# A perceiver block in one program: the folded queries on halves of the array's rows, the value products alternating between halves of its columns

## The chip, the cores and the metric

The kernel runs on one core of one Trainium2 chip. The metric is the device time of one execution in microseconds (us), taken over several executions; beside it stands one execution recorded by the hardware profiler. All data are fp32.

## What is computed

The reference is a two-layer perceiver on a latent `x` of 16 x 64 x 256 with a context of 16 x 1601 x 256: a cross attention that gathers samples, a self attention, a mixture of 8 experts, then a second cross attention, a state-space scan and a mixture of 32 experts. The change lies in the second cross attention alone:

```
def _L1_xattn_ref(x, context, Wq, Wk, Wv, Wk_ip, Wv_ip, Wo, bo):
    HEADS, DIM_HEAD, TEXT_LEN, SCALE = 16, 64, 77, 64 ** (-0.5)
    ctx_txt = context[:, :TEXT_LEN, :]
    ctx_img = context[:, TEXT_LEN:, :]                       # 1524 rows
    q = (x @ Wq).reshape(B, N, HEADS, DIM_HEAD)              # N = 64
    k = (ctx_txt @ Wk).reshape(B, TEXT_LEN, HEADS, DIM_HEAD)
    v = (ctx_txt @ Wv).reshape(B, TEXT_LEN, HEADS, DIM_HEAD)
    out = _attend(q, k, v)
    k_ip = (ctx_img @ Wk_ip).reshape(B, Li, HEADS, DIM_HEAD)
    v_ip = (ctx_img @ Wv_ip).reshape(B, Li, HEADS, DIM_HEAD)
    out_ip = _attend(q, k_ip, v_ip)
    out = out + out_ip
    return out @ Wo + bo
...
x = x + _L1_xattn_ref(_layernorm(x, axis=-1), ctx_1024, ...)
```

`_attend` is a softmax of `q k^T * SCALE` over the context rows, times `v`.

## The kernel before

**No keys and no values of the image rows are formed.** For a head, `q k^T = q Wk_ip^T ctx^T`, so the kernel first multiplies the 64 queries of the head with the head's 64 rows of `Wk_ip` and gets a folded query with 256 features ("fold"). The scores are then products of the raw context with the folded query. In the same way the probabilities are first multiplied with the raw context, which gives 256 features per query, and only then with the head's 64 columns of `Wv_ip` ("out").

**Tiling.** There are 16 batches and 16 heads. Two heads are taken together as a pair `hp`, with their 2 x 64 queries side by side as 128 columns. So there are 128 steps `n` (16 batches x 8 pairs). A step has 12 chunks of 128 context rows (the last has 116).

**One step (`Cross.step`, L1051), in the order in which TensorE (PE) gets it.** PE, VectorE (DVE) and ScalarE (ACT) work strictly in the order in which the Python code emits the work; nothing reorders it.

1. Three times, a PSUM bank `st` is filled with the scores of four chunks (L1068): 8 matmuls each, with the turned context `cT` as the stationary operand and the folded query `qf` as the moving one. DVE takes the maximum over the chunks (L1071, L1073). Between the second and the third bank, the normalised result of step n-2 is transposed (`turn_out`, L1042).
2. `out(n - 2)` (L1079): six matmuls into one bank `py`. Each head has a text product (77 rows of `vt` against `ptt`) and two image products (`wvi` against `ot`, one for each half of the 256 features). A head's `lhsT` has 64 columns, so head 0 uses the left half of the array's columns and writes partitions 0 to 63 of the bank, and head 1 the right half and partitions 64 to 127. All three products of head 0 are emitted, then all three of head 1.
3. The products of step n-1's probabilities with the context, in three parts of four chunks each (`product`, L1034). Between parts 0 and 1 stands the transpose of the maxima (L1088), between parts 1 and 2 the transpose that spreads them over all partitions (L1098) and, straight after it, `fold(n + 1)` (L1102).
4. ACT copies the spread maxima to `mc` (L1100) and the folded query to `qf` (L999); DVE subtracts `mc` from the three `st` banks (L1109, L1112) and ACT takes the exponentials (L1110, L1113). `qf` is needed by the first score matmul of step n+1.

**The fold.** `qbd` holds the scaled queries as a block diagonal: partitions 0 to 63 are the features of head 0 and are nonzero only in the columns of head 0's queries; partitions 64 to 127 and head 1 likewise. The other two blocks were set to zero once. A fold is therefore two full matmuls (128 rows, 128 columns, 128 moving columns), one for each half of the 256 features, into one bank, and one ACT copy of 256 columns.

**PSUM.** There are eight banks in two rings of four. `bank()` hands out the ring that nearly everything uses. `big()` hands out the ring of the score banks (L144); in this stage only L1065 takes from it, three a step. A bank that is handed out again must first have been read by all its readers; for a score bank the last of them is the subtraction on DVE (L1109, and for the third bank L1112).

**Around it.** Other work is woven into the steps by generators that are advanced at fixed places (`tick`, `mid`, `side`): the last gathers of the first cross attention, the self attention, the experts of the first layer, the state-space scan and the routing of the second layer.

An fp32 matmul shows in the trace as two passes, each with its own weight load. Where a row counts "x12" for `out`, these are the two passes of six matmuls; a fold is four passes.

Of the kernel before, what the change touches and what calls it, by code (L numbers as in the profile page):

```python
# [17 lines left out]
P = 128  # L18
B, S, D = 16, 64, 256
M = 1601  # L20
KC = D // P
# [13 lines left out]
H1, HD1, INNER, TEXT = 16, 64, 1024, 77  # L35
# [29 lines left out]
def perceiver_kernel(ctx: ExitStack, tc: tile.TileContext, a: dict, out: bass.AP):  # L65
    nc = tc.nc

    def mk(pool, shape, tag, dtype=F32, bufs=None):
        return pool.tile(list(shape), dtype, tag=tag, name=tag, bufs=bufs)
# [15 lines left out]
    def mm(o, pairs):  # L85
        for i, (l, r) in enumerate(pairs):
            nc.tensor.matmul(o, lhsT=l, rhs=r, start=i == 0, stop=i == len(pairs) - 1)  # L87
# [53 lines left out]
    def bank():  # L141
        return mk(pmm, [P, 512], "mm")

    def big():  # L144
        return mk(psc, [P, 512], "st")
# [9 lines left out]
    def load(pool, tag, src, shape, bufs=None):  # L155
        t = mk(pool, shape, tag, bufs=bufs)
        nc.sync.dma_start(out=t, in_=src)
        return t
# [46 lines left out]
    for t in range(TG):  # L205
        z = mk(const, [P, P], f"att{t}")
# [9 lines left out]
    qbds = [mk(xw, [P, NHP, 2, 2, S], f"qbd{i}") for i in range(2)]  # L216
# [50 lines left out]
    for j in range(2):  # L267
        r = slice(j * S, (j + 1) * S)
# [619 lines left out]
    class Cross:  # L888
# [98 lines left out]
        def fold(self, n):  # L987

            if n >= B * NHP:
                return  # L990
            b, hp = divmod(n, NHP)
            w = self.w[b, hp // 4]
            rhs = qbds[b // 2 % 2][:, hp, b % 2].rearrange("p h q -> p (h q)")
            pf = bank()
            for k in range(KC):
                nc.tensor.matmul(pf[:, k * P : (k + 1) * P], lhsT=w[:, hp % 4, k * P : (k + 1) * P], rhs=rhs,  # L996
                                 start=True, stop=True)
            qf = self.qf[n] = mk(self.xp, [P, KC, P], "qf", bufs=2)
            nc.scalar.copy(qf.rearrange("p c n -> p (c n)"), pf[:, : KC * P])  # L999

        def out(self, n):

            if n < 0:
                return
            b, hp = divmod(n, NHP)
            t, bb = divmod(b, 2)
            if t not in self.yt:
                self.yt[t] = mk(self.xp, [P, NHP, 2, S], "yt", bufs=2)
            ot = self.ot.pop(n)
            py = bank()  # L1010
            for h in range(2):
                r = slice(h * HD1, (h + 1) * HD1)
                cols = slice(hp * P + h * HD1, hp * P + (h + 1) * HD1)
                mm(py[r, :S], [(self.vt[b][:TEXT, cols], self.ptt[b][:TEXT, hp, r])]
                   + [(wvi[:, k, cols], ot[:, k, r]) for k in range(KC)])
            nc.scalar.copy(self.yt[t][:, hp, bb, :], py[:, :S])  # L1016

        def project(self, t):
# [484 lines left out]
    with tc.manual_schedule(engines={ET.PE, ET.DVE, ET.Activation}):  # L1503
# [43 lines left out]
        wvi = load(xw, "wvi", a["xwvi"].rearrange(kp, p=P), [P, KC, INNER])  # L1547
# [51 lines left out]
        i = 0  # L1599
# [104 lines left out]
```

## Time and profile before

| What | us |
|---|---|
| median of 10 executions | 3090.1 |
| lowest and highest of them | 3081.74 and 3097.48 |
| the profiled execution, its own time | 3084.45 |
| its span in the trace | 3082.6 |
| PE busy in the span | 2866.4 (93%) |
| stretch in which the 128 steps of the cross attention lie | about 850 to 2790 |

In rows of instructions, a form such as `128*64 128x64` stands for a matmul whose stationary operand covers 128 rows and 64 columns of the array and whose moving operand has 128 partitions and 64 columns. PEld is the loading of stationary operands, which has its own row and overlaps the matmuls. "Chain" rows give the start of a piece in us, its length, and what it was. The mean granted TensorE clock of the execution was 0.974 of full speed.

### The profile page before, as it was taken

The page shows a single profiled execution, that of the slowest core. Times are in us where ns is not written, and L with a number is a line of the kernel's source. Part 1 is how long each engine was busy: PE and PEld are TensorE (multiplying, and loading weights), DVE is VectorE, ACT ScalarE, POOL GpSimd, SP SyncE. Part 2 cuts the span into 40 slices and gives each one's busy share as a digit, 9 for nine tenths or more (in the row PEclk, how much of TensorE's full clock was granted, in tenths as well). Part 3 has the DMA queues.
Part 4 walks back from the last instruction along what each step waited for, and adds up shares of the span by engine and source line. Part 5 has one row for each costly group of instructions (what it writes and reads, how often), then busy time and mean ns, then how long its engine had stood idle before and what let it go on. Part 6 is the DMA issues. An engine that isn't in the chain of part 4 may idle for free.

```text
span 3082.6 us, 46371 instructions
## 1 busy us (share of the span) xinstructions
PE 2866.4 (93%) x17710; PEld 2367.0 (77%) x17710; DVE 1620.4 (53%) x4126; ACT 1017.3 (33%) x2353; POOL 809.3 (26%) x919
## 2 busy tenths in 40 slices
PE   7799999968799999988899999999999999998879
PEld 4454445646688898867799999999899999996666
DVE  3421223234365666655533457765686587656756
ACT  2343444312223223234233343333342433223421
POOL 0275446555345555200000000100020011002621
PEclk9899999988899999999999999999999999999999
DMA  6499876653312122120155221111121122004983
GB/s 210 116 191 197 241 210 192 182 145 109 111 28 71 30 68 70 47 70 31 61 164 189 66 73 50 60 53 53 35 84 56 38 68 69 8 1 153 287 234 114
DMA packets 338710, 326.19 MB, mean 106 GB/s; under 512 B 59301, under 2 KB 289097, under 8 KB 337977
## 3 DMA queue, kind: packets, MB, share of 16 engines
q1 hardware_dynamic: 186473, 226.04, 24.0%
q10 hardware_dynamic: 126640, 62.79, 7.7%
q0 software_dynamic: 25376, 34.39, 5.3%
q8 instruction: 141, 2.31, 0.3%
q14 instruction: 80, 0.66, 0.1%
HBM read 248.90 MB, written 74.22 MB: 105 GB/s over the span
## 4 chain that ended last, share of the span: by engine, by line
PE 77%; DVE 12%; DMA 5%; ACT 2%; issue 2%; POOL 1%; SPq 0%; ACTq 0%; DVEq 0%; POOLq 0%
PE st L87 32%; PE mm L1040 20%; PE mm L87 16%; PE mm L152 5%; DMA wg<-in_guT 2%; PE mm L996 2%; DMA tab<-kv 1%; PE mm L1026 1%; DVE mp L1071 1%; PE mm L965 1%; DMA cx<-in_ctx 1%; DVE pt L1109 1%; DVE hs L1275 1%; DMA g<-tab,ig 1%; PE mm L1088 1%
## 5 line engine op out<-in xcount | busy, mean ns | idle before, releaser
L427 POOL DMA_INDIRECT g<-tab,ig x640 | 610.9, 955 | 638.2 <-DVE ig L425 442.8
L1040 PE MATMUL mm<-cn,pt 128*128 128x257 f32 (+1 forms) x3072 | 740.5, 384 | 0.0
L87 PE MATMUL st<-qf,cT 128*128 128x128 f32 x6144 | 735.7, 277 | 0.9 <-ACT qf L999 0.9
L87 PEld LDWEIGHTS st<-qf,cT 128*128 128x128 f32 x6144 | 716.9, 193 | 5.9 <-ACT qf L999 2.4
L1040 PEld LDWEIGHTS mm<-cn,pt 128*128 128x128 f32 (+1 forms) x3072 | 554.0, 190 | 81.6 <-issue 0.8
L1071 DVE TENSOR_REDUCE mp<-st 128x128 f32<-128x512 f32 x384 | 260.7, 688 | 232.4 <-PE st L87 232.0
L87 PE MATMUL st<-wkv,cxt 128*128 128x512 f32 (+1 forms) x832 | 380.5, 602 | 0.6 <-ACT cxt L396 0.6
L1109 DVE TENSOR_TENSOR pt<-st,mc 128x512 f32<-128x512 f32 (+1 forms) x384 | 224.2, 640 | 133.4 <-ACT mc L1100 133.4
L87 PEld LDWEIGHTS st<-wkv,cxt 128*128 128x128 f32 (+1 forms) x832 | 151.0, 190 | 160.0 <-issue 158.1
L1110 ACT ACTIVATE pt<-pt 128x512 f32<-128x512 f32 (+1 forms) x384 | 208.1, 588 | 61.2 <-DVE pt L1109 60.9
L380 ACT COPY kv<-st 128x512 f32<-128x512 f32 (+1 forms) x208 | 120.9, 587 | 217.1 <-PE st L87 195.8
L1100 ACT COPY mc<-mm 128x128 f32<-128x128 f32 x128 | 34.1, 266 | 352.4 <-PE mm L1098 351.9
L1049 ACT COPY ot<-mm 128x256 f32<-128x256 f32 x128 | 47.5, 371 | 310.2 <-PE mm L152 309.7
L1090 DVE TENSOR_REDUCE xmx<-mm 128x1 f32<-128x128 f32 x128 | 37.4, 292 | 191.9 <-PE mm L1088 191.9
L87 PE MATMUL mm<-xt,w 128*128 128x256 f32 x512 | 122.8, 394 | 3.9 <-DVE act L815 3.8
L1281 POOL TENSOR_TENSOR ys<-ys,hc 128x512 f32<-128x512 f32 x64 | 81.5, 1274 | 161.1 <-DVE hc L1280 161.0
L87 PEld LDWEIGHTS mm<-xt,w 128*128 128x128 f32 x512 | 101.0, 199 | 28.8 <-issue 9.3
L1365 POOL DMA_INDIRECT xb<-xnd,row x55 | 55.2, 1004 | 241.6 <-PE mm L1026 199.8
L1016 ACT COPY yt<-mm 128x64 f32<-128x64 f32 x128 | 27.2, 213 | 253.5 <-PE mm L87 253.5
L459 DVE TENSOR_REDUCE smx<-sc 128x4 f32<-128x20 f32 x32 | 5.4, 168 | 167.4 <-ACT sc L457 167.4
L901 POOL MEMSET cn<- 128x12 f32 x16 | 1.8, 120 | 338.0 <-PE mm L1040 295.8
L815 DVE TENSOR_TENSOR act<-gl,mm 128x256 f32<-128x256 f32 x64 | 26.4, 418 | 107.6 <-ACT gl L814 107.5
(441 smaller groups left out, 3978.1 us busy)
## 6 DMA issues: line engine op xcount, KB each, us to landing
tab<-kv ACTq DMA_DIRECT2D x48, 1024.0 KB
w<-in_gate SPq DMA_DIRECT2D x62, 512.0 KB
cx<-in_ctx SPq DMA_DIRECT2D x48, 512.0 KB
cn<-in_ctx SPq DMA_DIRECT2D x16, 1408.0 KB
wg<-in_guT SPq DMA_DIRECT2D x87, 256.0 KB
wk<-in_xwkiT SPq DMA_DIRECT2D x32, 512.0 KB
w<-in_lin SPq DMA_DIRECT2D x31, 512.0 KB
wd<-in_down1T SPq DMA_DIRECT2D x87, 128.0 KB
```

Source lines behind the costliest of these rows:

```text
L87: nc.tensor.matmul(o, lhsT=l, rhs=r, start=i == 0, stop=i == len(pairs) - 1)
L152: nc.tensor.transpose(t[:ncol, i, :rows], b, ident[:rows, :rows])
L380: nc.scalar.copy(kv[:w, :, c, :], pk[:w].rearrange("p (h e) -> p h e", h=H0))
L427: nc.gpsimd.indirect_dma_start(out=gf[:, (half * n + s) * 4 * HD0 : (half * n + s + 1) * 4 * HD0], out_offset=None, in_=tables[j], in_offs ...
L996: nc.tensor.matmul(pf[:, k * P : (k + 1) * P], lhsT=w[:, hp % 4, k * P : (k + 1) * P], rhs=rhs, start=True, stop=True)
L1040: nc.tensor.matmul(po, lhsT=pt[:w, c, :], rhs=cn[:w, c, :], start=c == 0, stop=c == NCH - 1)
L1049: nc.scalar.copy(ot, tp[:, :KC, :])
L1071: nc.vector.tensor_reduce(mp_[:, i, :], s.rearrange("p c n -> p n c"), AX.X, ALU.max)
L1109: nc.vector.tensor_tensor(o, st[i][:, :m, :], mc.to_broadcast([P, m, P]), ALU.subtract)
L1110: nc.scalar.activation(o, o, AF.Exp)
L1281: nc.gpsimd.tensor_tensor(y, y, hc, ALU.add)
L1365: nc.gpsimd.indirect_dma_start(out=x, out_offset=None, in_=xnd, in_offset=bass.IndirectOffsetOnAxis(ap=tb.row[:, i : i + 1], axis=0))
```

## The change

`fold` and `out` are rewritten; nothing else differs.

```
         def fold(self, n):
...
-            rhs = qbds[b // 2 % 2][:, hp, b % 2].rearrange("p h q -> p (h q)")
-            pf = bank()
+
+            pf = [z[:, : KC * S].rearrange("p (k q) -> p k q", q=S) for z in (bank(), big())]
             for k in range(KC):
-                nc.tensor.matmul(pf[:, k * P : (k + 1) * P], lhsT=w[:, hp % 4, k * P : (k + 1) * P], rhs=rhs,
-                                 start=True, stop=True)
+                for h in range(2):
+                    r = slice(h * HD1, (h + 1) * HD1)
+                    nc.tensor.matmul(pf[h][:, k, :], lhsT=w[r, hp % 4, k * P : (k + 1) * P],
+                                     rhs=qbds[b // 2 % 2][r, hp, b % 2, h, :], start=True, stop=True)
             qf = self.qf[n] = mk(self.xp, [P, KC, P], "qf", bufs=2)
-            nc.scalar.copy(qf.rearrange("p c n -> p (c n)"), pf[:, : KC * P])
+            for h in range(2):
+                nc.scalar.copy(qf[:, :, h * S : (h + 1) * S], pf[h])
 
         def out(self, n):
...
             py = bank()
+            pairs = []
             for h in range(2):
                 r = slice(h * HD1, (h + 1) * HD1)
                 cols = slice(hp * P + h * HD1, hp * P + (h + 1) * HD1)
-                mm(py[r, :S], [(self.vt[b][:TEXT, cols], self.ptt[b][:TEXT, hp, r])]
-                   + [(wvi[:, k, cols], ot[:, k, r]) for k in range(KC)])
+                pairs.append([(self.vt[b][:TEXT, cols], self.ptt[b][:TEXT, hp, r])]
+                             + [(wvi[:, k, cols], ot[:, k, r]) for k in range(KC)])
+
+            for i in range(KC + 1):
+                for h in range(2):
+                    l, m = pairs[h][i]
+                    nc.tensor.matmul(py[h * HD1 : (h + 1) * HD1, :S], lhsT=l, rhs=m, start=i == 0, stop=i == KC)
             nc.scalar.copy(self.yt[t][:, hp, bb, :], py[:, :S])
```

In `fold`, the two full matmuls become four: for each half of the features one for each head, with that head's 64 rows of the array, all 128 columns and 64 moving columns. The zero blocks of `qbd` are no longer read here (the text scores still read them). The two heads write two banks, one from each ring, so the ring of the score banks now hands out four banks a step. The one ACT copy of 256 columns becomes two of 2 x 64 columns, one for each bank.

In `out`, the same six matmuls are emitted in another order: text product of head 0, text product of head 1, then the two image products in the same alternation.

## The prediction

> **What bounds the kernel now.** I read the page's busy shares first, then the busy time by stretches, then the chain of waits inside one step, and last the order of time around the two places that change.
>
> ```profile
> PE 2866.4 (93%) x17710; PEld 2367.0 (77%) x17710; DVE 1620.4 (53%) x4126; ACT 1017.3 (33%) x2353; POOL 809.3 (26%) x919
> ```
>
> ```profile
> 1180.00:1500.00 320.00, 288.99 (x2019) 258.32 (x2018) 187.59 (x539) 103.23 (x247) 51.93 (x62) 0.96 0.18 55
> ...
> 1840.00:2300.00 460.00, 457.42 (x3426) 420.77 (x3425) 312.34 (x663) 167.22 (x410) 39.04 (x62) 1.00 0.19 58
> 2300.00:2790.00 490.00, 484.81 (x3578) 443.14 (x3577) 317.02 (x746) 161.67 (x398) 29.38 (x45) 1.00 0.12 38
> ```
>
> Columns: stretch, its length, busy us of PE, PEld, DVE, ACT, POOL, then the granted clock. In the second half of the cross attention PE is busy for 457.4 of 460.0 and 484.8 of 490.0 us at full clock. The loosest stretch (1180 to 1500) still has 289 of 320. So what the change adds to PE's own time in a step, or takes from it, reaches the end nearly whole, 128 times. In the chain of one step (start, length, what):
>
> ```profile
> 1508.75 1.79 PE st L87 x16
> 1510.54 0.66 PE mm L87 x12
> 1511.20 1.94 PE mm L1040 x8
> ...
> 1515.43 0.11 PE mm L1098
> 1515.54 0.45 PE mm L996 x4
> 1515.99 1.74 PE mm L1040 x8
> ```
>
> Everything here is PE. Sixteen full passes take 1.79, that is 0.112 each. The fold (L996) is four such passes, 0.45, with no gap around it. `out` (the L87 row with x12) is twelve passes of a quarter of the size in 0.66. And the eight passes of `product` take 1.74 behind the fold but 1.94 behind `out`, though they are the same work.
>
> **What `out` pays today for halves of the array.** The order of time around it:
>
> ```profile
> 1510.26 0.28 PE L87 MATMUL st<-qf,cT 128*128 128x128 f32 x1
> ```
>
> ```profile
> 1510.46 0.33 PE L87 MATMUL mm<-ptt,vt 77*64 77x64 f32 x2
> 1510.63 0.22 PE L87 MATMUL mm<-ot,wvi 128*64 128x64 f32 x1
> 1510.64 0.27 PE L87 MATMUL mm<-ptt,vt 77*64 77x64 f32 x1
> 1510.69 0.22 PE L87 MATMUL mm<-ot,wvi 128*64 128x64 f32 x1
> 1510.74 0.22 PE L87 MATMUL mm<-ptt,vt 77*64 77x64 f32 x1
> 1510.75 0.45 PE L87 MATMUL mm<-ot,wvi 128*64 128x64 f32 x6
> ```
>
> The last full pass starts at 1510.26. A full pass would follow 0.11 later; the first pass on half of the columns starts at 1510.46, so 0.09 is lost, and its weights were not loaded ahead (64 columns at the rate of 128 in 0.11: 0.06). Entry: 0.15. Exit: 1.94 - 1.74 = 0.20. And the halves already run at the same time: head 0 starts at 1510.46, head 1 at 1510.64 while head 0 is still going (1510.69 and 1510.74 belong to different heads). The 0.66 is thus 0.15 entry, 0.17 that head 1 lags behind head 0, and six passes of 0.056 (1510.63 to 1510.69) = 0.34.
>
> **Term 1, the alternation in `out`.** Same six matmuls, same entry and exit. What can go is the lag: head 1's first pass is now second in the queue, and the pairs at 1510.63/1510.64 and 1510.74/1510.75 show that two passes on different halves can start within 0.01. Gain at most 0.17, at least 0 (if starting both cold costs what it saves). I take 0.17: 128 x 0.17 = **-22 us**; bounds -22 to 0.
>
> **Term 2, the fold on PE.** Removed: two full matmuls, four passes, 0.45. Added: four matmuls, eight passes of 64 rows, 128 columns and 64 moving columns. How short can such a pass be? The rows nearest to it have full weights and even fewer moving columns:
>
> ```profile
> 1512.97 0.53 PEld L635 LDWEIGHTS mm<-hb,hp 128*128 128x128 f32 x4
> 1513.08 0.52 PE L635 MATMUL mm<-hb,hp 128*128 128x15 f32 x4
> ...
> 1513.42 1.61 PEld L1040 LDWEIGHTS mm<-cn,pt 128*128 128x128 f32 x8
> ```
>
> Four loads from 1512.97 to 1513.42: 0.11 each with only 15 moving columns. Loading 128 columns is the floor. Fewer rows do not shorten it: in the rows of `out`, a load of 77 rows and 64 columns takes 134 ns, one of 128 rows and 64 columns 138. So halving the moving columns saves nothing but the tail of the last pass, 0.056; eight passes at 0.11 come back to four times 0.11 only where the two heads' loads run side by side.
>
> Do they, and does switching to half rows cost what half columns cost? No row of this trace has half rows at work among full passes. Bounds: no switch cost and side by side, 0.39 to 0.45 against 0.45, that is -7 to 0 us. Switch cost as in `out` and one after the other: entry 0.15 plus 0.06, because 128 rather than 64 columns load uncovered, 0.21; eight passes 0.90, less the tail 0.056; exit 0.20; 1.25 against 0.45, 127 x 0.80 = +102 us. The nearest row is `out`, which shows both a switch cost and halves side by side. I take both from it: 0.21 + 4 x 0.112 - 0.056 + 0.20 = 0.80 against 0.45: 127 x 0.35 = **+44 us**. (The first of the 128 folds lies ahead of the steps.)
>
> The Trainium skill pulls both ways here. "TensorEngine Tiling (Array Packing)", section Overview, Theoretical Speedup, gives up to 2x for a dimension of 64 or less; as an estimate from that page the fold would fall from 0.45 to 0.22 and gain 29 us. The loads of 0.11 above contradict it for this shape. Its section Key Properties says that changing the tiling mode, not just the tile, drains TensorE, which speaks against the change; the 0.15 and 0.20 around `out` agree for half columns, and no row here shows it for half rows.
>
> **Term 3, ACT.** One copy of 256 columns (L999, 373 ns) becomes two of 128. L1100 copies 128 columns from PSUM in 266 ns:
>
> ```profile
> L1100 ACT COPY mc<-mm 128x128 f32<-128x128 f32 x128 | 34.1, 266 | 352.4 <-PE mm L1098 351.9
> ```
>
> So 0.53 instead of 0.37, +0.16 a step, or 20 us on an engine with 33% busy. What hides it: `qf` is needed only when part 2 of `product` is through, 1.74 behind the fold. Without that cover it would cost the 20 us. Queued behind the copies on ACT are the exponentials, which now begin up to 0.5 later; `product` wants them a step later. The short wait that could grow is `out` on the copy of `ot` behind them, 5.1 us over seven cases today. I take 0 to 5, +1.
>
> **Term 4, the ring of score banks.** Three a step out of four left one bank free: the first score bank of step n+1 was the free one, and the second reused the first of step n. Now the fold takes the fourth, so the first bank of n+1 is the first of n and must wait for its subtraction on DVE. Queued behind that wait on PE are all 24 score matmuls, then `out`. Mostly the subtraction is through: half of the steps have over 1.1 us to spare. Where side work sits ahead on DVE it isn't:
>
> ```profile
> 1876.14 3.73 PE L87 MATMUL st<-qf,cT 128*128 128x128 f32 x32
> ...
> 1876.72 1.75 DVE L1109 TENSOR_TENSOR pt<-st,mc 128x512 f32<-128x512 f32 x3
> ```
>
> The three subtractions take 1.75, so the first ends near 1877.4, 1.27 after PE started the bank that would now wait. Setting the start of each step's first score bank beside the end of that subtraction, ten of 127 steps are short, by 5.7 us together; a fold that is 0.35 longer gives part of it back and leaves 2.7. With 0.15 a case for the semaphore and the first load it is 4 us. Bounds 0 to 7; I take **+3 us**.
>
> **Sum.** -22 + 44 + 1 + 3 = +26 us. Against the profiled execution, 3084.45, that is 3110; this one lay 5.7 below the median, so against the median of 3090.1 it is **3116 us**. 0.2% or 6 us is about what a measurement can tell from no change.
>
> **The rivals.**
>
> *Half rows cost no switch* (other side). Place: entry and exit of the fold. If full and half rows mix as freely as two full passes do, term 2 is -7 to 0, and -22 - 4 + 4 leaves 3068. For it: the rows' halves need no new destination columns, and no row here shows a drain for them. Against: `out`, 128 times the same 0.15 and 0.20. It decides once the fold's surplus is below the lag that `out` saves, 0.17 a step, half of what `out` pays today.
>
> *Half rows switch, and their weight loads queue up.* Then the fold costs 1.25: +102 - 22 + 4, 3174. For it: the full passes have one load every 0.11 throughout. Against: the loads of `out` overlap across halves.
>
> *The alternation does not do what it says.* The halves overlap already; if starting both at once only moves the wait, term 1 is 0: 44 + 4, 3138.
>
> **How the numbers follow.** The forecast (3116, own range 3098 to 3134, the switch cost of 0.41 a third off either way) gets 0.58; no switch cost on the rows 0.18; loads queueing 0.14; no gain from alternating 0.10. The predicted time is the likeliest's. The range takes in the forecast, the no-gain case and the no-switch case, whose bounds reach 3062, and stops at 3142; it leaves out queueing loads and small tails, near 0.18. Faster by over 0.2% is the no-switch case and little else: 0.18. Within 0.2%: the forecast with half of the switch cost, 0.05. Slower: the rest, 0.77.
>
> **What would show it.** Right: `product` behind the fold takes 1.94 instead of 1.74, and the fold's own piece of the chain grows from 0.45 to near 0.6; `out` shrinks from 0.66 to near 0.49, with the two heads' first passes within 0.01; a few waits of score matmuls on L1109, none of weight on `qf`. Wrong: 1.74 behind the fold (no switch), or the fold's piece above 0.9 (loads queue), or `out` still at 0.66. If PE's waits on DVE in this stage pass 10 us, term 4 was mis-sized.

## The result: 0.7% slower, and the profile after

| What | before | after |
|---|---|---|
| median, us | 3088.95 (28 executions) | 3111.59 (8 executions) |
| lowest and highest | 3081.74 and 3097.48 | 3108.19 and 3114.09 |
| span of the profiled execution | 3082.6 | 3113.0 |
| PE busy in the span | 2866.4 (93%) | 2900.5 (93%) |

The ratio of after to before is 1.0073, with a 95% interval from 1.0064 to 1.0082: 22.6 us slower, where 26 was forecast.

Busy time by stretches in after (stretch, length, busy us of PE, PEld, DVE, ACT, POOL, granted clock):

```profile
1180.00:1500.00 320.00, 289.86 (x2066) 254.91 (x2065) 183.26 (x510) 102.92 (x263) 58.44 (x68) 0.96 0.19 55
...
1840.00:2300.00 460.00, 458.03 (x3503) 412.25 (x3502) 305.58 (x653) 168.82 (x435) 35.59 (x57) 1.00 0.18 57
2300.00:2790.00 490.00, 489.16 (x3744) 440.70 (x3743) 328.32 (x758) 166.09 (x439) 32.23 (x49) 1.00 0.13 41
```

PE is as full as before at the same clock, while the loads (PEld) are a little less busy. It has more to get through, not more to wait for. The chain of one step in after (start, length, what; a fold's passes stand as `mm` for the first bank and `st` for the second):

```profile
1912.64 0.50 PE mm L1024 x12
1913.14 1.94 PE mm L1049 x8
...
1916.92 0.11 PE mm L1107
1917.03 0.25 PE mm L998
1917.28 0.01 PE st L998
1917.29 0.11 PE mm L998
1917.39 0.01 PE st L998
1917.40 0.10 PE mm L998
1917.51 0.01 PE st L998
1917.51 0.10 PE mm L998
1917.62 0.01 PE st L998
1917.62 1.94 PE mm L1049 x8
```

`out` has shrunk from 0.66 to 0.50. The fold has grown from 0.45 to 0.60: its first piece is 0.25 instead of 0.11, each later pass of the first head costs 0.10 to 0.11, and the second head adds 0.01 each time, so the two heads' rows do run side by side. And the eight passes of `product` behind the fold take 1.94 instead of 1.74, as they always did behind `out`. A step thus loses 0.15 + 0.20 at the fold and gains 0.16 at `out`.

The order of time at `out` in after shows that the lag is gone; all four text passes and all eight image passes now stand together:

```profile
1912.57 0.34 PE L1024 MATMUL mm<-ptt,vt 77*64 77x64 f32 x4
1912.73 0.40 PE L1024 MATMUL mm<-ot,wvi 128*64 128x64 f32 x8
1913.07 0.48 PE L1049 MATMUL mm<-cn,pt 128*128 128x257 f32 x1
```

### The profile page after: what moved, and what is told of

It reads as the page before. It is cut to its first block, busy times and chain, and to the rows that moved or that the text cites. A ratio compares the mean times of both kernels' runs of the same rounds, so it can differ in the third digit from the quotient of the medians.

```text
span 3113.0 us, 47465 instructions
## 1 busy us (share of the span) xinstructions
PE 2900.5 (93%) x18222; PEld 2365.8 (76%) x18222; DVE 1627.9 (52%) x4126; ACT 1026.2 (33%) x2481; POOL 813.2 (26%) x919
## 4 chain that ended last, share of the span: by engine, by line
PE 79%; DVE 10%; DMA 4%; ACT 2%; issue 2%; POOL 1%; SPq 0%; ACTq 0%; DVEq 0%; POOLq 0%
PE st L87 33%; PE mm L1049 21%; PE mm L87 14%; PE mm L152 5%; PE mm L998 2%; PE mm L1024 2%; DMA tab<-kv 1%; DMA wg<-in_guT 1%; PE mm L1035 1%; POOL g L427 1%; DMA g<-tab,ig 1%; PE mm L965 1%; DVE mp L1080 1%; DVE cv L471 1%; PE mm L1097 1%
## 5 line engine op out<-in xcount | busy, mean ns | idle before, releaser
L1049 PE MATMUL mm<-cn,pt 128*128 128x257 f32 (+1 forms) x3072 | 754.8, 389 | 0.0
L1118 DVE TENSOR_TENSOR pt<-st,mc 128x512 f32<-128x512 f32 (+1 forms) x384 | 224.2, 640 | 133.3 <-ACT mc L1109 133.3
L998 PEld LDWEIGHTS mm<-qbd,wk 64*128 64x128 f32 x512 | 66.6, 187 | 35.6 <-issue 31.9
```

Source lines behind the costliest of these rows:

```text
L998: nc.tensor.matmul(pf[h][:, k, :], lhsT=w[r, hp % 4, k * P : (k + 1) * P], rhs=qbds[b // 2 % 2][r, hp, b % 2, h, :], start=True, stop=True)
L1049: nc.tensor.matmul(po, lhsT=pt[:w, c, :], rhs=cn[:w, c, :], start=c == 0, stop=c == NCH - 1)
L1118: nc.vector.tensor_tensor(o, st[i][:, :m, :], mc.to_broadcast([P, m, P]), ALU.subtract)
```

## The experiments

Three measures are used. The ratio to before, with its interval, comes from executions on the same chip. The pieces of the chain show one step. The third is a sum that a single trace gives: the time from the first score matmul of step 48 to the last one of step 127, some 80 steps. It is 1148.7 us in before and 1161.9 in after, 0.165 a step more. In e3, e5 and e11, where the fold and `out` take as long as in before, it is 1148.6 to 1148.9. In these steps the granted clock was full in every trace but two: e7 and e10 have one stretch each of 3.4 us at half the clock (at 2487 and 2163 us). By an estimate from its length it costs 1.7 us, and e8 and e10, traces of one and the same kernel, differ by 1.5. This third measure is needed because e5 to e8 ran on another chip, on which before took 3395 us. There steps 0 to 31, among which the gathers still run, took 579 to 607 us against 437 in before's trace, and work ahead of the steps some 155 us more; the last 80 steps were as fast as on the first chip.

**e1: the new order in `out` alone.** The edit is the `out` half of the change.

> Before with the new order of the value products alone; the fold stays two full matmuls into one bank. My theory (head 1 lags head 0 by 0.17 us today, alternating removes the lag): 0.17 x 128 = 22 us faster than before, about 3067; the piece of `out` in the chain shrinks from 0.66 to 0.50, and the product behind it stays at 1.94. Rival (starting both halves at once only moves the wait): no change, 3089, and `out` stays near 0.66.

Measured: ratio 0.9954 (0.9941 to 0.9968), 3069.2 us beside 3084.2 for before, 15 us faster. The chain of e1:

```profile
1523.62 0.50 PE mm L1021 x12
1524.12 1.94 PE mm L1046 x8
...
1528.02 0.45 PE mm L996 x4
1528.46 1.74 PE mm L1046 x8
```

`out` is 0.50 as in after, the fold and what follows it as in before. The last 80 steps take 1137.2, 0.144 a step less. The theory holds; of the 0.16 that `out` lost, nine tenths reach the end in these steps. At that rate all 128 would give 18 us, the edge of what was measured (10 to 18, by the interval). In steps 0 to 31 of this one trace nothing is left of the gain (437.3 against 437.0). Most of that is the granted clock. The first two steps of before and of e1 (last three columns: granted clock, DMA share, GB/s):

```profile
849.60:870.30 20.70, 18.65 (x132) 17.09 (x132) 10.82 (x25) 3.13 (x9) 7.55 (x8) 0.97 0.05 10
845.00:867.90 22.90, 20.86 (x133) 19.29 (x133) 10.83 (x25) 3.13 (x9) 8.51 (x9) 0.86 0.06 12
```

With the clock at 0.86 instead of 0.97 they took 2.2 us longer; steps 30 and 31 took 1.3 longer, at 0.94 instead of 1.00. Besides, PE waited 13.8 us in steps 0 to 31 instead of 12.1, for copies and maxima of other engines. Steps 2 to 29 gained 3.2.

**e2: the new fold alone.** The edit is the `fold` half of the change.

> Before with the new fold alone; the value products keep their old order. My theory (a switch to half rows and back costs 0.21 and 0.20 a fold, the weight loads of the two heads run side by side): 127 x 0.35 = 44 us slower than before, about 3133; fold piece 0.60, product behind it 1.94. Rival (the loss of the whole change comes from the second bank and the second ACT copy, the row halves being free): this kernel is then slower only by what they cost and the chain shows it as waits of score matmuls on DVE or ACT, with the product behind the fold at 1.74.

Measured: ratio 1.0149 (1.0135 to 1.0163), 3130.1 us, 46 us slower. The last 80 steps take 1173.7, 0.313 a step more. Its chain has `out` at 0.66, the fold at 0.59, with a first piece of 0.25 as in after, and the product behind it at 1.94:

```profile
1510.30 0.66 PE mm L87 x12
1510.96 1.94 PE mm L1043 x8
...
1514.86 0.25 PE mm L998
...
1515.45 1.94 PE mm L1043 x8
```

In the steps the two halves of the change add up: +0.313 - 0.144 = +0.169, against 0.165 in after. The totals do so less well: 46 - 15 = 31 us, where 22.6 were measured. Each of them is uncertain by some 3 to 4 us, and the alternation, which alone gave 15 us, gives 23 on top of the new fold (from 1.0149 to 1.0073).

**e3: the banks and the copies without the half rows.**

```
-            pf = bank()
+            pf = (bank(), big())
...
-                nc.tensor.matmul(pf[:, k * P : (k + 1) * P], lhsT=w[:, hp % 4, k * P : (k + 1) * P], rhs=rhs,
+                nc.tensor.matmul(pf[k][:, :P], lhsT=w[:, hp % 4, k * P : (k + 1) * P], rhs=rhs,
...
-            nc.scalar.copy(qf.rearrange("p c n -> p (c n)"), pf[:, : KC * P])
+            for k in range(KC):
+                nc.scalar.copy(qf[:, k, :], pf[k][:, :P])
```

> Before with full matmuls in the fold, but one bank from each ring, one for each half of the features, and two ACT copies of 128 columns: the bank and copy side of the change without half rows. My terms 3 and 4 gave 4 us slower (0 to 12). The trace of after shows first score banks that begin up to 0.92 us before the subtraction of the step before has ended, so the wait of term 4 seems not to be there: then 0 to 2 us slower, 3089 to 3091, and no wait of PE on DVE's L1109. Rival (bank and copies make the loss of the fold): some 40 us slower, 3130.

Measured: ratio 1.0001 (0.9991 to 1.0012); the last 80 steps take 1148.9 against 1148.7. The second bank and the second copy cost nothing that can be told from zero, and the product behind this fold takes 1.74:

```profile
1532.44 0.22 PE mm L996 x2
1532.67 0.22 PE st L996 x2
1532.89 1.74 PE mm L1041 x8
```

With e2 this puts the whole loss of the fold on the half rows.

**e4: the fold's heads one after the other.** In after, the two `for` lines of the fold are exchanged, so that both matmuls of head 0 precede head 1's.

> After with the four matmuls of the fold in another order: both of head 0, then both of head 1. If row halves look ahead as the column halves of before did (head 1 begins with head 0's fourth load, three loads late), head 1 lags by 3 x 0.112 = 0.34: 127 x 0.34 = 43 us slower than after, about 3154. If the halves do not look ahead at all, 0.45 and 57 us, 3169. If order does not matter on rows, 3112.

Measured: ratio 1.0094 (1.0079 to 1.0110), 3112.8 us; the last 80 steps take 1162.4 against after's 1161.9. Of the three cases named beforehand the last one holds: the order does not matter here, and the 43 us that were named first were a miss. The loads at one fold:

```profile
1901.33 0.18 PEld L998 LDWEIGHTS mm<-qbd,wk 64*128 64x128 f32 x1 [0.28 <-PE mm L1049]
1901.35 0.18 PEld L998 LDWEIGHTS st<-qbd,wk 64*128 64x128 f32 x1
```

Head 1's first load (the `st` row), emitted fifth, starts 14 ns after head 0's first (1901.333 and 1901.347). So halves can start together although their work is emitted in turn, and the lag in `out` needed a cause of its own; e5, e11 and e12 look for it.

**e5: the wait moved to the front of `out`.** In before, each head's products in the order image, image, text.

```
-                mm(py[r, :S], [(self.vt[b][:TEXT, cols], self.ptt[b][:TEXT, hp, r])]
-                   + [(wvi[:, k, cols], ot[:, k, r]) for k in range(KC)])
+                mm(py[r, :S], [(wvi[:, k, cols], ot[:, k, r]) for k in range(KC)]
+                   + [(self.vt[b][:TEXT, cols], self.ptt[b][:TEXT, hp, r])])
```

> Before with each head's three value products in the order image, image, text instead of text, image, image; the heads still one after the other. e4 showed halves of the rows starting 0.01 us apart though emitted in turn, while in before the halves of the columns start 0.17 apart. Theory: what held head 1 back in before was the wait for `ot` that stands on head 0's second product; TensorE does not look past it. Here the wait stands on the first product, so head 1 should start within 0.02 of head 0, `out` takes 0.50 in the chain and the time is that of e1, some 15 us under before. Rival (columns look ahead less far than rows): the lag stays near 0.17, `out` near 0.66, and the time is that of before.

Measured: ratio 0.9989 (0.9975 to 1.0003); the last 80 steps take 1148.9. From the first to the last pass of `out` it is 0.513 (median over the steps), as in before (0.511). The theory of the wait falls.

**e11: a bank for each head in `out`, heads in turn.** In before, `py` becomes two banks, each head writes its own and has its own ACT copy.

> Before with each head's value products in a bank of their own (two ACT copies), heads still one after the other: all text and image products of head 0, then head 1's. If head 1 lags in before because both halves write one bank, it now starts within 0.02 us of head 0 and `out` takes 0.50 in the chain. If it lags because TensorE looks only some passes ahead, the lag stays 0.17 and `out` 0.66.

One execution, 3093.9 us; the last 80 steps take 1148.6. Its order of time at `out` is before's:

```profile
2212.34 0.33 PE L87 MATMUL mm<-ptt,vt 77*64 77x64 f32 x2
2212.51 0.22 PE L87 MATMUL mm<-ot,wvi 128*64 128x64 f32 x1
2212.51 0.27 PE L87 MATMUL mm<-ptt,vt 77*64 77x64 f32 x1
```

Head 1's first text pass still comes 0.17 after head 0's. A shared bank is not the cause.

**e12: fewer passes ahead of head 1.** In before, `out` without its text products, heads in turn.

> Before without the text product in `out` (the text part of the attention's output is left out), heads one after the other: four passes of head 0 ahead of head 1 instead of six, as in the fold of e4. If TensorE looks a fixed number of passes ahead, head 1 lags by some 0.06 (one load) or less instead of 0.17. If halves of the columns are held back for another reason, the lag stays at three loads, 0.17.

One execution, 3063.2 us. All eight passes form one piece of 0.46, and in the trace the first loads of the two heads are 13 ns apart (2201.444 and 2201.457), where before has 171:

```profile
2201.13 0.39 PE L87 MATMUL st<-qf,cT 128*128 128x128 f32 x2
2201.45 0.46 PE L87 MATMUL mm<-ot,wvi 128*64 128x64 f32 x8
```

With four passes of head 0 emitted first, head 1 starts at once, on half columns (e12) as on half rows (e4); with six it starts with head 0's fourth load (before, e5, e11), whether the text products stand first (before, e11) or last (e5). The nanoseconds of the traces suggest one rule for both cases. In before head 1's first load (1510.634) comes 4 ns after head 0's third pass has started (1510.630), when three passes of head 0 are still to start; in e12 and e4 it comes 12 ns after head 0's first pass has started (2201.445 in e12), again with three still to start. With four still to start (before, from 1510.571 on) it did not come. So in these runs TensorE starts the other half past three passes that have not begun, and not past four. That is why alternating gained something in `out` and makes no difference in the fold. It also corrects the description ahead of the prediction, by which PE works strictly in the order emitted: between halves it does not, and head 1's first text pass (1510.636) starts ahead of head 0's last three image passes (1510.690 and later).

**e6 and e9: `out` on the whole array.** In before, both heads' columns at once; the two off-diagonal blocks of the result are not used.

```
-            for h in range(2):
...
+            cols = slice(hp * P, (hp + 1) * P)
+            mm(py[:, :P], [(self.vt[b][:TEXT, cols], self.ptt[b][:TEXT, hp, :])]
+               + [(wvi[:, k, cols], ot[:, k, :]) for k in range(KC)])
-            nc.scalar.copy(self.yt[t][:, hp, bb, :], py[:, :S])
+            for h in range(2):
+                r = slice(h * HD1, (h + 1) * HD1)
+                nc.scalar.copy(self.yt[t][r, hp, bb, :], py[r, r])
```

> Before with the value products on the whole array: three full matmuls (128 columns of vt or wvi for both heads, 128 moving columns), of which only the two diagonal blocks are used and copied by two ACT copies; nothing in the steps switches the array any more. From last pass before to second pass of product after: 0.112 + 5 x 0.112 + 0.112 + 0.219 = 1.00 us against 1.19 in before and 1.02 in e1, and the product behind it takes 1.74. Theory (the switches cost 0.15 and 0.20): as fast as e1 or up to 3 us faster, 3067. Rival (the 1.94 behind `out` is due to something else, such as the bank of `py` or ACT's copy): the product stays at 1.94 and the time at 3090 or above.

> The kernel of e6 again: e6 to e8 ran on a chip on which before took 3395 us, with the loss in the first 40% of the program (the gathers), so the totals there hide the change. On the last 96 steps e6 took 0.18 us a step less than before. Theory: 18 to 24 us faster than before where before takes near 3085. Rival: the 31 us of e6 repeat.

Measured: e6 0.9897 (0.9876 to 0.9917) on the slower chip, e9 0.9940 (0.9926 to 0.9954), 3067.0 us beside 3085.7 for before. The last 80 steps take 1136.0 in both. The chain of e9:

```profile
1912.77 0.67 PE mm L87 x6
1913.44 1.74 PE mm L1040 x8
```

Six full passes take 0.67, as long as the twelve quarter-size ones did, and the product behind them is back at 1.74. This shows that the 1.94 belonged to the switch of the array's shape. Doing twice the arithmetic in `out` without a switch is 19 us faster than before's version with one. The larger gain of e6 on the other chip arose in steps 0 to 31 (579 us there, 596 in e5) and was not followed up.

**e7: the new fold right behind `out`.** In after, `self.fold(n + 1)` is moved from behind L1107 to behind `self.out(n - 2)`.

> After with the fold of the next step moved from behind L1107 to right behind `out`, so that the array goes from halves of columns straight to halves of rows and back to whole once: one exit and one entry fewer if a change between two kinds of halves costs only one drain. Theory (drain and uncovered first load at every change of shape): 0.19 a step less than after, 127 x 0.19 = 24 us, about 3087. Rival (between halves of either kind the change is free): 0.34 a step less, 43 us, about 3069. If the place of the fold does not matter: 3112.

Measured on the slower chip: ratio 1.0001 (0.9984 to 1.0017). The last 80 steps take 1149.3, 0.158 a step less than after: near the 0.19 of the theory, far from the 0.34 of the rival. With the stretch of half clock taken off, it would be 0.18. The chain of e7:

```profile
2208.15 0.50 PE mm L1024 x12
2208.65 0.25 PE mm L998
...
2209.24 1.94 PE mm L1049 x8
```

The first piece of the fold takes 0.25 behind half columns, as it does in after behind a full pass. So going from half columns to half rows costs as much as going in from the whole array; what the new place saves is one way back, one of four changes of shape a step.

**e8 and e10: the fold on quarters, right behind `out`.** As e7, with the fold's matmuls split once more:

```
             for k in range(KC):
+                for m in range(2):
...
+                        c0 = k * P + m * HD1
+                        nc.tensor.matmul(pf[h][m * HD1 : (m + 1) * HD1, k, :], lhsT=w[r, hp % 4, c0 : c0 + HD1],
+                                         rhs=qbds[b // 2 % 2][r, hp, b % 2, h, :], start=True, stop=True)
```

> As e7, but the fold as eight matmuls on quarters of the array (64 rows of the head, 64 columns of the features, 64 moving columns; still one bank a head). Loads of 64 columns take half of the time, four quarters run side by side: four passes of 0.056 instead of four of 0.112. Theory: one drain between halves and quarters (0.15), one back (0.20), `out` plus fold some 0.07 a step under e1 and 0.40 under after: about 3060, the fastest so far. Rival (the quarters do not all run side by side): 0.22 a step more, about 3088.

> The kernel of e8 again, for its total where before takes near 3085. On the last 80 steps e8 took 0.19 us a step less than before. Theory: 15 to 24 us faster than before. Rival (what e8 gains in the steps is given back elsewhere, as its total on the other chip says): no change.

Measured: e8 0.9999 (0.9981 to 1.0016) on the slower chip, where steps 0 to 31 took 607 us; e10 0.9941 (0.9928 to 0.9955), 3068.2 us. The last 80 steps take 1133.7 and 1135.2, 0.17 to 0.19 a step less than before; e10's is the one with the stretch of half clock. All sixteen passes of a fold take 0.39 in the chain of e10 (1912.18 to 1912.57), 0.20 of it until the first has ended, so four quarters run side by side:

```profile
1911.68 0.50 PE mm L1026 x12
1912.18 0.20 PE mm L1000
1912.38 0.01 PE st L1000
...
1912.57 1.94 PE mm L1051 x8
```

Here smaller stationary operands pay for themselves. That they do so only because the fold stands beside `out` and shares its way back is an estimate: at the old place, with a way back of 0.20 of their own, they would take 0.59 against 0.45; this was not run. Why nothing of this reached the end on the slower chip stays open.

Three kernels beat both before and after: e1 (0.9954), e9 (0.9940) and e10 (0.9941). Their intervals overlap; none leaves the whole array more than once a step for `out` and the fold, and before leaves it once too.

## Why the prediction was right

**Term 1, the alternation (-22 us).** The mechanism held and the size at its place too. From the last pass before `out` to the second pass behind it, the median went from 1.188 to 1.024 us, 0.164 x 128 = 21 us. Alone it gave 15 us (e1), on top of the new fold 23 (after against e2). What was left out is that not all of it reaches the end: the prediction let every step count in full, and e1's last 80 steps passed on 0.144 of 0.164.

**Term 2, the fold (+44 us).** From the transpose ahead of it to the second pass of the product behind it, the median went from 0.773 to 1.113 us: 0.340 x 127 = 43 us; e2 gave 46. Both choices made from `out`, a switch cost and halves side by side, were right. Inside, two sizes were off and cancelled, which was luck: the entry was put at 0.21 and is 0.14 (the first piece of 0.25 less a pass of 0.11), and the shorter last pass, put at -0.056, is not there. A pass of 64 moving columns against 128 stationary ones takes 272 ns in the trace of after, a full one 275. The exit is the 0.20 that was read from `out`. The floor of 0.11 a load, which spoke against any gain, is in the chain.

**Term 3, ACT (+1 us).** Two copies of 266 and 271 ns, as expected from `mc`; hidden, as e3 shows.

**Term 4, the ring of score banks (+3 us).** This step was wrong. It said that the first score bank of step n+1 "is the first of n and must wait for its subtraction on DVE". In after nothing on PE waits for L1118, and here PE starts the first score bank of the next step before the subtraction has begun:

```profile
1891.52 1.73 PE L87 MATMUL st<-qf,cT 128*128 128x128 f32 x14
1891.76 1.75 DVE L1118 TENSOR_TENSOR pt<-st,mc 128x512 f32<-128x512 f32 x3
```

In seven of 127 steps the scores start before that subtraction has ended, by up to 0.92 us. So that bank isn't the one being subtracted from. The one bank that is free by then is the fold's, emptied by the two copies that the scores wait for anyway; that the pool hands it out is an inference from this, not read off. e3 measures the price: none. Without terms 3 and 4 the sum is -22 + 44 = 22, and 22.6 were measured; with uncertainties of some 3 us that is no proof of either.

**The rivals.** No switch on the rows: out, by 1.94 behind the fold. Loads queueing up: out, by the second head's 0.01. No gain from alternating: out, by e1.

## What to carry to other kernels

A matmul on part of the array has to pay for the change of shape twice, going in and coming back: here 0.34 us an excursion, as much as three full passes. Half the moving columns save nothing where loading the stationary operand sets the pace; what shortens a pass is fewer stationary columns. So either stay on the whole array and compute blocks that are thrown away, or gather all the partial work of a step into one excursion, with the halves emitted in alternation; a change of shape inside it is not free (e7).

## What the runs showed of the hardware that was not expected

- TensorE starts another half of the array out of the emitted order. With four passes emitted ahead of it, it came 13 ns late (e12; 14 in e4), with six 171 ns late (before, e5, e11), in both cases once three passes ahead of it were still to start. Five passes were not tried, and what sets the limit stays open.
- Half rows and half columns cost much the same to enter and leave (0.14 and 0.20 against 0.15 and 0.20), and a change between the two is not free (e7: the first piece of the fold is 0.25 there too).
- A stretch of 3.4 us at half the granted clock can fall into one execution and not into another of the same kernel (e10 and e8); by an estimate from its length it costs 1.7 us.
- Four quarters of the array ran side by side: sixteen passes in 0.39 us (e10), the entry among it.
- The same program took 3085 us on one chip and 3395 on another, the difference lying ahead of step 32, where the gathers run (granted clock in steps 0 to 31: 0.89 in e5, 1.00 in before); why was not looked into. The last 80 steps of e5 there (1148.9) and of before here (1148.7) were equal.
